# Part of the gram chains of images 1 to 5 moved from VectorE to ScalarE and GpSimd

## The chip, the cores and the metric

The kernel runs on one core of a Trainium2 chip. A core has five engines that run their own queues in order: TensorE (PE, matrix products into PSUM), VectorE (DVE), ScalarE (ACT), GpSimd (POOL) and SyncE (SP), which here only issues transfers. They wait for each other through semaphores. The metric is the device time of one execution in microseconds (us).

## The reference

A batch of 16 images of 64 channels and 128 x 128 pixels, in fp32, passes four layers of the form `x = x + f(gn(x))`, where `gn` is a group norm over 32 groups of two channels:

```
layer 0: f = conv_w @ (gram(v) @ v),  gram(v) = v v^T / (H W)   per image
layer 1: f = |scharr_x(v)| + |scharr_y(v)|                       3x3, per channel
layer 2: f = 3x3 convolution of the time-shifted v, plus bias
layer 3: f = clip(leaky(bn(conv1x1(conv3x3(v)))), 0, 255)        bn over all images
```

Layer 0 is linear in `x` once the 64 x 64 gram matrix of an image is known. So the kernel folds the norm, the gram product and `conv_w` into one 128 x 128 matrix (`abd`, two copies of a 64 x 64 block on the diagonal), and finds the statistics of the next norm (`co1`) from the gram matrix as well. That is a chain of small matrix products and small elementwise operations for each image, the gram chain. It must be done before layer 1 of the image can begin.

## The kernel before

**Stages.** The work is cut into steps of four quarters (`q` = 0 to 3). In a step each live stage does one slab of 16 of the 128 rows of one image. `Gram` (L407) loads `x` as `xr`, has ACT copy it into `xw` and sums the gram matrix into the PSUM tile `pg`. `Front` (L450) multiplies the image by `abd` on PE (`po`), normalizes it on ACT into `xh`, and does the Scharr filters of layer 1 (`sobel`, L527): on DVE `u` and `e` at the start of the quarters 0, four operations in quarter 1, one each in 2 and 3, with ACT's two `Abs` in between. `Layer2` (L625) normalizes its slab on ACT (`v`, in quarter 1), then POOL takes the border columns: four `edges` of 64 x 8 and two `v` of 128 x 9, also in quarter 1. In quarters 3 and 0 DVE forms a difference of rows (`d`), of which POOL's DMAs make shifted copies (`qd`). PE convolves: `one`, then the two halves of `two`, in quarters 2 and 3. DVE adds `edges` and `c` to `two` in quarter 0 of the next step. `Layer3` (L773) is alike, with ACT instead of POOL for `qd`.

**What runs when.** `starts` (L861) gives Front's image 0 step 15, Layer2's step 25 and Layer3's step 35, and each next image 8 steps more. The gram matrices of images 1 to 6 are made at double pace, one every 4 steps (L874), so they lie early, while Front works on images 0 to 2. `EARLY` is 3. In the last part, after the statistics of layer 3 are complete, the kernel reads all of `y` and `x3` again and writes the output.

**Order.** The stages record their instructions through `InOrder` (L63), which keeps each engine's instructions in program order; nearly all of them bear its line, L73, in the profile, so they are told apart by their tiles. At the end of each quarter `tick` (L252) lets every live chain go on to its next `yield`. A chain's operations of a quarter therefore stand in each engine's queue behind the stages' operations of that quarter.

**The gram chain** (L301) is a generator. One tick holds either PE's product or the small operations that follow from it; for image 1 (and 0) the yields under `if b > 1` fall away, so that both share a tick. `small_product` (L177) issues four small matmuls into `bank`, one PSUM bank that all chains share through `sm` (L187). The names in order: `gs` is `pg` out of PSUM; `g` the gram matrix of the image, with `st0` and `junk0` its means and squares; `rstd` (L257) makes the group's reciprocal deviation `r` (its `Sqrt`, `sd`, on ACT, the rest on DVE); `vv` holds vectors of means, `rw` their products as rows, `cs` the centred gram matrix, `rc` the scaled weights; `r2`, `wbd`, `ad` and `abd` are the folded matrix; `pp`, `av`, `pk`, `bias`, `st1` and `t` lead to the statistics of layer 0's output; `rstd` again, and `co` (the tile is `co1`) is what Front needs. `coefficients` (L278) is the shorter chain that layers 2 and 3 use, with the same `bank`. All small operations of both are on DVE before the change, apart from `sd`.

Of the kernel before, what the change touches and what calls it, by code (L numbers as in the profile page):

```python
# [12 lines left out]
ALU = mybir.AluOpType  # L13
AX = mybir.AxisListType

B, C, H, W = 16, 64, 128, 128
P = 128
HW = H * W
# [4 lines left out]
EARLY = 3  # L23
# [85 lines left out]
def tile_kernel(ctx: ExitStack, tc: tile.TileContext, x, cw_h, w2_t, b2, wbin_t, w1_t, b1, gamma, beta, consts, out):  # L109
    nc = tc.nc  # L110
    pe, dve, act, sp, pool = (InOrder(tc, e) for e in (nc.tensor, nc.vector, nc.scalar, nc.sync, nc.gpsimd))
# [9 lines left out]
    def k(name):  # L121
        return kc[:, AT[name][0]:AT[name][1]]

    def load_const(src, shape, name):
        t = cpool.tile(shape, F32, name=name)
        nc.sync.dma_start(t, src)
        return t

    cwh = load_const(cw_h, [P, C], "cwh")
# [39 lines left out]
    def sv(name, n=1):  # L169
        return small.tile([P, n], F32, tag=name, name=name)  # L170
# [6 lines left out]
    def small_product(dst, wt, src):  # L177

        for o in (1 - last[0], last[0]):
            pe.matmul(dst[cols(o)], wt[:, cols(o)], src, start=True, stop=True)  # L180
        last[0] = o
# [5 lines left out]
    def sm(n, rows=P):  # L187
        if n > 8:
            return bank[0:rows, P:P + n]
        turn[0] = (turn[0] + 1) % 16  # L190
        return bank[0:rows, 8 * turn[0]:8 * turn[0] + n]
# [9 lines left out]
    wbd = wpool.tile([P, P], F32, name="wbd")  # L201
# [55 lines left out]
    def rstd(mE, eps):  # L257

        me = sv("me", 2)
        dve.tensor_copy(me, mE)  # L260
        nv = sv("nv")
        dve.scalar_tensor_tensor(nv, me[:, 0:1], me[:, 0:1], me[:, 1:2], op0=ALU.mult, op1=ALU.subtract)
        var = sv("var")
        dve.tensor_scalar(var, nv, -1.0, eps, op0=ALU.mult, op1=ALU.add)
        sd = sv("sd")
        act.activation(sd, var, AF.Sqrt)
        yield
        r0 = sv("r0")
        dve.reciprocal(r0, sd)

        e = sv("e")
        dve.scalar_tensor_tensor(e, var, r0, r0, op0=ALU.mult, op1=ALU.mult)
        dve.tensor_scalar(e, e, -0.5, 1.5, op0=ALU.mult, op1=ALU.add)
        r = sv("r")
        dve.tensor_mul(r, r0, e)
        return r, me[:, 0:1]
# [23 lines left out]

    def gram_chain(b, pg):  # L301

        gs = stp.tile([P, C + 1], F32, tag="gs", name=f"gs_{b}", bufs=1)
        dve.tensor_copy(gs, pg)
        if b > 1:
            yield
        gd = sm(C + 1)
        small_product(gd, k("same"), gs)
        yield
        g = stp.tile([P, C + 1], F32, tag="g", name=f"g_{b}", bufs=1)  # L310
        dve.tensor_scalar_mul(g, gd, 1.0 / HW)
        mu = g[:, C:C + 1]
        st = sv("st0", 2)
        dve.tensor_copy(st[:, 0:1], mu)
        junk0 = stp.tile([P, C], F32, tag="junk0", name=f"junk0_{b}", bufs=1)
        dve.scalar_tensor_tensor(
            junk0, g[:, 0:C], 1.0, k("Id"), op0=ALU.mult, op1=ALU.mult, accum_out=st[:, 1:2]
        )
        if b > 1:
            yield  # L320
        pm = sm(2)
        small_product(pm, k("gavg"), st)
        yield
        r, mean = yield from rstd(pm, GN_EPS)

        vv = sv("vv", 5)
        dve.tensor_scalar_mul(vv[:, 0:1], mu, -1.0)
        dve.tensor_sub(vv[:, 1:2], mu, mean)
        dve.tensor_copy(vv[:, 2:3], mu)
        dve.tensor_sub(vv[:, 3:4], mu, mean)  # L330
        dve.tensor_scalar_mul(vv[:, 4:5], mean, -1.0)
        if b > 1:
            yield
        pr = sm(2 * P, rows=2)
        pe.matmul(pr[:, 0:P], vv[:, 0:2], k("hsame"), start=True, stop=True)
        pe.matmul(pr[:, P:2 * P], vv[:, 2:4], k("hsame"), start=True, stop=True)
        yield
        rw = stp.tile([2, 2 * P], F32, tag="rw", name=f"rw_{b}", bufs=1)
        dve.tensor_copy(rw, pr)
        if b > 1:  # L340
            yield
        pc = sm(C)
        pe.matmul(pc, rw[:, 0:P], rw[:, P:P + C], start=True, stop=True)
        yield

        cs = stp.tile([P, 2, C], F32, tag="cs", name=f"cs_{b}", bufs=1)
        for s in range(2):
            dve.tensor_add(cs[:, s, :], pc, g[:, 0:C])
        rc = stp.tile([P, C], F32, tag="rc", name=f"rc_{b}", bufs=1)
        dve.tensor_scalar(rc, cwh, r, 0.5, op0=ALU.mult, op1=ALU.mult)  # L350
        csf = cs.rearrange("p s c -> p (s c)")
        if b > 1:
            yield
        pq = sm(C)
        small_product(pq, csf, rc)
        yield
        r2 = sv("r2")
        dve.tensor_mul(r2, r, r)
        for s in range(2):
            rows = slice(s * C, (s + 1) * C)  # L360
            dve.tensor_scalar_mul(wbd[rows, rows], pq[rows], r2[rows])
        ad = stp.tile([P, C], F32, tag="ad", name=f"ad_{b}", bufs=1)
        dve.scalar_tensor_tensor(ad, pq, r2, k("Id"), op0=ALU.mult, op1=ALU.add)
        abd = stp.tile([P, P], F32, tag="abd", name=f"abd_{b}", bufs=EARLY + 3)
        dve.tensor_add(abd, wbd, k("I"))
        if b > 1:
            yield
        pd = sm(C + 3)
        small_product(pd[:, 0:C], csf, ad)
        small_product(pd[:, C:C + 2], abd, vv[:, 2:4])  # L370
        small_product(pd[:, C + 2:C + 3], wbd, vv[:, 4:5])
        yield
        pp = stp.tile([P, 2, C], F32, tag="pp", name=f"pp_{b}", bufs=1)
        for s in range(2):
            dve.tensor_mul(pp[:, s, :], pd[:, 0:C], ad)
        av = sv("av", 3)
        dve.tensor_copy(av, pd[:, C:C + 3])
        if b > 1:
            yield
        pk = sm(1)  # L380
        small_product(pk, pp.rearrange("p s c -> p (s c)"), k("q"))
        yield
        bias = sv("bias")
        dve.tensor_copy(bias, av[:, 2:3])
        st1 = sv("st1", 2)
        dve.tensor_add(st1[:, 0:1], av[:, 0:1], bias)
        t = sv("t1")
        dve.scalar_tensor_tensor(t, av[:, 1:2], av[:, 1:2], pk, op0=ALU.mult, op1=ALU.subtract)
        dve.scalar_tensor_tensor(
            st1[:, 1:2], st1[:, 0:1], st1[:, 0:1], t, op0=ALU.mult, op1=ALU.subtract  # L390
        )
        if b > 1:
            yield
        pm = sm(2)
        small_product(pm, k("gavg"), st1)
        yield
        r, mean = yield from rstd(pm, GN_EPS)

        co = stp.tile([P, 4], F32, tag="co1", name=f"co1_{b}", bufs=EARLY + 3)
        dve.tensor_copy(co[:, 0:1], r)  # L400
        dve.tensor_sub(co[:, 1:2], bias, mean)
        dve.tensor_mul(co[:, 1:2], co[:, 1:2], r)
        dve.reciprocal(co[:, 2:3], r)
        dve.tensor_copy(co[:, 3:4], mean)
        lead[b] = abd, co

    class Gram:  # L407
# [5 lines left out]
        def at(self, i, q):  # L413
# [29 lines left out]
            if n == 6:  # L443
                chains.append(gram_chain(b, self.pg))
# [466 lines left out]
    for step in range(steps):  # L911
        for q in range(4):
# [13 lines left out]
            for b in range(B):  # L926
                at, n = pace[b]
                for m in range(n):
                    v = 4 * n * (step - at) + n * q + m
# [101 lines left out]
```

## Time and profile before

| | |
|---|---|
| median of 3 runs | 2827.53 us (2825.04 to 2830.61) |
| the profiled execution's own time | 2829.05 us |
| its span | 2827.3 us |
| busy share of the span: PE, DVE, ACT, POOL | 79%, 78%, 75%, 31% |
| mean of one 128x1 operation of a chain on DVE | 0.13 to 0.16 us, issued 0.07 apart where independent |
| one large Scharr operation on DVE | 1.22 to 1.38 us |
| chains of images 1 to 5: `gs` at | 80.9, 128.4, 176.1, 236.7, 297.6 us |
| their last `co` at | 115.2, 186.7, 247.9, 310.5, 381.1 us |

The profile is of one execution. Its slices give each engine's busy share in tenths over 40 equal parts of the span, and below them the clock that the chip granted TensorE. A table of windows gives the same in microseconds between chosen times: length, then busy time and number of instructions for PE, PEld (weight loads), DVE, ACT and POOL, then PE's clock, the share in which the DMA engines were busy, and GB/s. The list of waits says which engine, before which tile, stood still for whom: the sum in us, how often, and the longest. A timeline has one row per instruction or run of equal ones: start, duration, engine, operation and tiles, and in brackets the idle time ahead of it and what ended it.

### The profile page before, as it was taken

The numbers are of one execution on the slowest core, as the hardware profiler recorded it, in microseconds if no ns is written. First come the engines' busy times: TensorE is split into PE (matmuls) and PEld (weight loads), VectorE is DVE, ScalarE is ACT, GpSimd is POOL, SyncE is SP. The second block draws the span as 40 slices with busy tenths as digits, with TensorE's granted clock in tenths as the row PEclk, the third lists the DMA queues.
The fourth block names the chain that finished last, engine by engine and source line by source line (L and its number), as shares of the span: only waits on it lengthen the run. The fifth ranks groups of instructions, "written<-read, shape, count | busy, mean of one in ns | idle before, by whom it ended". The sixth has DMA issues, their size and how long they took to land. (4 is left out here: it accounts for less than half of the span.)

```text
span 2827.3 us, 46297 instructions
## 1 busy us (share of the span) xinstructions
PE 2241.5 (79%) x14772; PEld 1157.1 (41%) x14772; DVE 2200.4 (78%) x3758; ACT 2120.5 (75%) x3171; POOL 884.3 (31%) x1326
## 2 busy tenths in 40 slices
PE   4568899999999999999999999999999995000000
PEld 2333444545453535363646363566666641000000
DVE  3999999898989898989898989999996434333332
ACT  4666779888888888888888888998997666333332
POOL 1035433343434343434343434454444300000000
PEclk8678999999999999999999999999999997555555
DMA  6788978888888888888888877888877668999999
GB/s 166 192 219 227 235 199 237 213 232 205 229 209 224 213 221 215 220 216 223 215 221 216 220 183 191 207 207 213 208 209 186 156 201 285 419 420 420 420 420 391
DMA packets 688880, 685.95 MB, mean 243 GB/s; under 512 B 61744, under 2 KB 590144, under 8 KB 688640
## 3 DMA queue, kind: packets, MB, share of 16 engines
q1 hardware_dynamic: 662656, 614.42, 73.7%
q0 software_dynamic: 24576, 68.12, 9.8%
q8 instruction: 119, 1.95, 0.3%
q14 instruction: 121, 0.99, 0.1%
q10 hardware_dynamic: 1408, 0.46, 0.1%
HBM read 346.23 MB, written 268.44 MB: 217 GB/s over the span
## 5 line engine op out<-in xcount | busy, mean ns | idle before, releaser
L73 PE MATMUL two<-d,w 128*64 128x508 f32 (+2 forms) x2560 | 894.2, 588 | 5.8 <-DVE d L73 5.8
L73 PE MATMUL two<-d,wi 128*64 128x508 f32 (+3 forms) x1536 | 620.1, 577 | 0.0
L73 POOL DMA_DIRECT2D qd<-d x512 | 269.8, 529 | 870.8 <-issue 318.4
L73 PE MATMUL two<-qd,pk 128*64 128x512 f32 (+1 forms) x1024 | 520.3, 589 | 3.2 <-DMA qd<-d 2.1
L73 POOL TENSOR_SCALAR edges<-v,co 64x8 f32<-64x8 f32 x512 | 348.8, 681 | 357.9 <-ACT v L73 248.7
L73 PEld LDWEIGHTS two<-d,w 128*64 128x64 f32 x2560 | 305.3, 136 | 285.5 <-issue 194.7
L73 PE MATMUL po<-x,abd 128*64 128x512 f32 x1024 | 369.8, 629 | 61.6 <-ACT xh L73 60.6
L73 DVE TENSOR_TENSOR d<-v 128x512 f32<-128x512 f32 (+1 forms) x512 | 345.9, 678 | 75.3 <-issue 36.0
L73 PE MATMUL one<-v,w 128*64 128x508 f32 (+2 forms) x1600 | 394.7, 578 | 0.0
L73 PE MATMUL one<-v,wi 128*64 128x508 f32 (+3 forms) x1536 | 391.4, 593 | 0.0
L73 ACT COPY qd<-d 64x512 f32<-64x512 f32 x512 | 315.3, 616 | 30.1 <-DVE d L73 23.7
L73 DVE SCALAR_TENSOR_TENSOR e<-e 128x1032 f32<-128x1032 f32 (+1 forms) x256 | 312.7, 1222 | 0.0
L73 ACT ACTIVATE xh<-po,co 128x128 f32<-128x128 f32 (+1 forms) x480 | 275.1, 621 | 40.8 <-PE po L73 38.8
L73 DVE SCALAR_TENSOR_TENSOR y<-two,c 128x1024 f32<-128x1024 f32 x128 | 155.8, 1217 | 132.0 <-ACT v L73 44.2
L73 PEld LDWEIGHTS two<-d,wi 128*64 128x64 f32 x1536 | 195.7, 136 | 145.2 <-issue 97.7
L73 POOL TENSOR_SCALAR v<-v,kc 128x9 f32<-128x9 f32 x256 | 249.7, 988 | 11.9
L73 PEld LDWEIGHTS one<-v,w 128*64 128x64 f32 x1600 | 171.9, 137 | 159.3 <-issue 97.5
L73 ACT ACTIVATE v<-x,co 128x512 f32<-128x512 f32 (+2 forms) x368 | 234.9, 704 | 0.0
L73 PEld LDWEIGHTS one<-v,wi 128*64 128x64 f32 x1536 | 163.0, 139 | 154.2 <-issue 110.1
L73 ACT ACTIVATE u<-u 128x1024 f32<-128x1024 f32 x128 | 135.5, 1058 | 96.7 <-DVE u L73 96.3
L73 DVE SCALAR_TENSOR_TENSOR u<-xh 128x1170 f32<-128x1170 f32 x128 | 175.5, 1371 | 12.2 <-ACT xh L73 9.8
L73 PEld LDWEIGHTS po<-x,abd 128*64 128x64 f32 x1024 | 110.8, 140 | 174.3 <-ACT xh L73 93.1
(154 smaller groups left out, 3476.0 us busy)
## 6 DMA issues: line engine op xcount, KB each, us to landing
xr<-in_x SPq DMA_DIRECT2D x128, 512.0 KB, 6.6
x<-in_x SPq DMA_DIRECT2D x256, 256.0 KB, 4.2
x_d<-u SPq DMA_DIRECT2D x512, 128.0 KB, 3.6
y_d<-y SPq DMA_DIRECT2D x512, 128.0 KB, 4.3
x_d<-x SPq DMA_DIRECT2D x496, 128.0 KB, 2.5
qd<-d POOLq DMA_DIRECT2D x256, 130.0 KB, 3.1
qd<-d POOLq DMA_DIRECT2D x256, 129.8 KB, 3.6
v<-x_d SPq DMA_DIRECT2D x448, 72.1 KB, 3.0
```

What stands on the lines that cost most here:

```text
L73: return self.tc.keep_in_program_order(call(*args, **kwargs))
```

## The change

For the chains of images 1 to 5 (`fill`; `2 * EARLY` is 6) the operations that read PSUM and are plain copies or scalings go to ACT: `gs`, `g`, `rw`, the two halves of `wbd`, `av`. Fifteen operations on small SBUF tiles go to POOL: `st0`, five of `vv`, `rc`, `r2`, `abd`, `bias`, the first half of `st1`, four of `co`. `junk0`, `cs`, `ad`, `pp`, `t`, the second half of `st1`, the reciprocal of `co` and all of `rstd` stay on DVE. The ticks and the order of the program are the same. The chains of image 0 and of images 6 to 15 are built as before.

```diff
...
 
     def gram_chain(b, pg):
 
+
+        fill = 1 <= b < 2 * EARLY
+        v, copy = (pool, act.copy) if fill else (dve, dve.tensor_copy)
+
+        def scaled(dst, src, by):
+            if fill:
+                act.mul(dst, src, by)
+            else:
+                dve.tensor_scalar_mul(dst, src, by)
+
         gs = stp.tile([P, C + 1], F32, tag="gs", name=f"gs_{b}", bufs=1)
-        dve.tensor_copy(gs, pg)
+        copy(gs, pg)
         if b > 1:
             yield
         gd = sm(C + 1)
         small_product(gd, k("same"), gs)
         yield
         g = stp.tile([P, C + 1], F32, tag="g", name=f"g_{b}", bufs=1)
-        dve.tensor_scalar_mul(g, gd, 1.0 / HW)
+        scaled(g, gd, 1.0 / HW)
         mu = g[:, C:C + 1]
         st = sv("st0", 2)
-        dve.tensor_copy(st[:, 0:1], mu)
+        v.tensor_copy(st[:, 0:1], mu)
         junk0 = stp.tile([P, C], F32, tag="junk0", name=f"junk0_{b}", bufs=1)
         dve.scalar_tensor_tensor(
             junk0, g[:, 0:C], 1.0, k("Id"), op0=ALU.mult, op1=ALU.mult, accum_out=st[:, 1:2]
...
         r, mean = yield from rstd(pm, GN_EPS)
 
         vv = sv("vv", 5)
-        dve.tensor_scalar_mul(vv[:, 0:1], mu, -1.0)
-        dve.tensor_sub(vv[:, 1:2], mu, mean)
-        dve.tensor_copy(vv[:, 2:3], mu)
-        dve.tensor_sub(vv[:, 3:4], mu, mean)
-        dve.tensor_scalar_mul(vv[:, 4:5], mean, -1.0)
+        v.tensor_scalar_mul(vv[:, 0:1], mu, -1.0)
+        v.tensor_sub(vv[:, 1:2], mu, mean)
+        v.tensor_copy(vv[:, 2:3], mu)
+        v.tensor_sub(vv[:, 3:4], mu, mean)
+        v.tensor_scalar_mul(vv[:, 4:5], mean, -1.0)
         if b > 1:
             yield
         pr = sm(2 * P, rows=2)
...
         pe.matmul(pr[:, P:2 * P], vv[:, 2:4], k("hsame"), start=True, stop=True)
         yield
         rw = stp.tile([2, 2 * P], F32, tag="rw", name=f"rw_{b}", bufs=1)
-        dve.tensor_copy(rw, pr)
+        copy(rw, pr)
         if b > 1:
             yield
         pc = sm(C)
...
         for s in range(2):
             dve.tensor_add(cs[:, s, :], pc, g[:, 0:C])
         rc = stp.tile([P, C], F32, tag="rc", name=f"rc_{b}", bufs=1)
-        dve.tensor_scalar(rc, cwh, r, 0.5, op0=ALU.mult, op1=ALU.mult)
+        v.tensor_scalar(rc, cwh, r, 0.5, op0=ALU.mult, op1=ALU.mult)
         csf = cs.rearrange("p s c -> p (s c)")
         if b > 1:
             yield
...
         small_product(pq, csf, rc)
         yield
         r2 = sv("r2")
-        dve.tensor_mul(r2, r, r)
+        v.tensor_mul(r2, r, r)
         for s in range(2):
             rows = slice(s * C, (s + 1) * C)
-            dve.tensor_scalar_mul(wbd[rows, rows], pq[rows], r2[rows])
+            scaled(wbd[rows, rows], pq[rows], r2[rows])
         ad = stp.tile([P, C], F32, tag="ad", name=f"ad_{b}", bufs=1)
         dve.scalar_tensor_tensor(ad, pq, r2, k("Id"), op0=ALU.mult, op1=ALU.add)
         abd = stp.tile([P, P], F32, tag="abd", name=f"abd_{b}", bufs=EARLY + 3)
-        dve.tensor_add(abd, wbd, k("I"))
+        v.tensor_add(abd, wbd, k("I"))
         if b > 1:
             yield
         pd = sm(C + 3)
...
         for s in range(2):
             dve.tensor_mul(pp[:, s, :], pd[:, 0:C], ad)
         av = sv("av", 3)
-        dve.tensor_copy(av, pd[:, C:C + 3])
+        copy(av, pd[:, C:C + 3])
         if b > 1:
             yield
         pk = sm(1)
         small_product(pk, pp.rearrange("p s c -> p (s c)"), k("q"))
         yield
         bias = sv("bias")
-        dve.tensor_copy(bias, av[:, 2:3])
+        v.tensor_copy(bias, av[:, 2:3])
         st1 = sv("st1", 2)
-        dve.tensor_add(st1[:, 0:1], av[:, 0:1], bias)
+        v.tensor_add(st1[:, 0:1], av[:, 0:1], bias)
         t = sv("t1")
         dve.scalar_tensor_tensor(t, av[:, 1:2], av[:, 1:2], pk, op0=ALU.mult, op1=ALU.subtract)
         dve.scalar_tensor_tensor(
...
         r, mean = yield from rstd(pm, GN_EPS)
 
         co = stp.tile([P, 4], F32, tag="co1", name=f"co1_{b}", bufs=EARLY + 3)
-        dve.tensor_copy(co[:, 0:1], r)
-        dve.tensor_sub(co[:, 1:2], bias, mean)
-        dve.tensor_mul(co[:, 1:2], co[:, 1:2], r)
+        v.tensor_copy(co[:, 0:1], r)
+        v.tensor_sub(co[:, 1:2], bias, mean)
+        v.tensor_mul(co[:, 1:2], co[:, 1:2], r)
         dve.reciprocal(co[:, 2:3], r)
-        dve.tensor_copy(co[:, 3:4], mean)
+        v.tensor_copy(co[:, 3:4], mean)
         lead[b] = abd, co
 
     class Gram:
```

In the built program the order on PE and SP is the same as before, instruction by instruction. On ACT, `gs` stands behind two copies of `xw` and before `xh`; `g` behind a copy of `xw` and before the two `Abs`; `rw` and `wbd` behind two `xh`; `av` behind the square of the slab and before `v`. In chain 1 `g` stands behind the square of the slab, `rw` and `wbd` behind a copy of `xw`, `av` behind two `xh`. On POOL, in chains 3 to 5, the order of one chain among the stages' work is:

```
edges x4, v x2, co x4 of the chain before, st0, qd x2, qd x2, vv x5, edges x4, v x2, qd x2, qd x2,
rc, edges x4, v x2, r2, abd, qd x2, qd x2, edges x4, v x2, bias, st1, qd x2, qd x2, ...
```

In chains 1 and 2 no `edges`, `v` or `qd` lie between, but for one set of `edges` and `v` before `bias` of chain 2. On DVE, `ad` waits for ACT, beside PE and POOL.

## The prediction

> **What bounds the kernel now.** I read three things, from coarse to fine. First the slices of the page, which say where one engine is full:
>
> ```profile
> PE   4568899999999999999999999999999995000000
> DVE  3999999898989898989898989999996434333332
> ACT  4666779888888888888888888998997666333332
> PEclk8678999999999999999999999999999997555555
> ```
>
> A slice is 70.7 us. VectorE (DVE) is full in slices 2 to 5 while TensorE (PE) is at 5 to 8; from slice 6 (about 350 us) PE is full at full clock. The five chains of images 1 to 5 run from 80.9 us (first `gs`) to about 381 us (last `co`), so the change lies in the stretch in which DVE sets the pace. The same cut finer, with each engine's busy time, then the granted PE clock:
>
> ```profile
> 80.00:120.00 40.00, 18.02 (x134) 7.82 (x130) 37.02 (x74) 26.62 (x37) 0.20 (x1) 0.59 0.66 167
> 120.00:167.00 47.00, 26.87 (x371) 15.70 (x369) 43.91 (x77) 31.72 (x46) 0.20 (x1) 0.66 0.84 202
> 167.00:240.00 73.00, 60.56 (x656) 30.03 (x652) 67.08 (x125) 45.89 (x63) 43.35 (x50) 0.91 0.92 235
> 240.00:305.00 65.00, 54.59 (x515) 26.80 (x516) 60.41 (x128) 45.88 (x68) 32.07 (x42) 0.89 0.95 239
> 305.00:370.00 65.00, 58.56 (x496) 26.27 (x494) 57.41 (x117) 52.31 (x78) 30.30 (x40) 0.95 0.84 217
> 370.00:430.00 60.00, 60.00 (x316) 23.42 (x314) 58.07 (x122) 50.01 (x81) 21.96 (x32) 1.00 0.79 206
> ```
>
> DVE (third) is busy 93% and more until 305 us, PE (first) is close behind from 167 us on, and GpSimd (POOL, fifth), idle before 167 us, then has a half to 60% of its time taken. What a delay of PE costs there is nearly what a delay of DVE costs. What DVE waits for between 80 and 380 us:
>
> ```profile
> DVE gs L73 <- PE pg L73: 6.8, 5, 1.8
> DVE d L73 <- POOL v L73: 5.9, 5, 1.6
> DVE d L73 <- issue: 2.7, 1, 2.7
> DVE u L73 <- ACT u L73: 2.6, 2, 1.3
> ```
>
> So the only engine it repeatedly waits for within a step is POOL, whose `edges` and `v` come once per step. Last, the timeline of DVE, POOL and PE in one step of chain 3:
>
> ```profile
> 196.68 0.14 DVE L73 TENSOR_SCALAR vv<-me 128x1 f32<-128x1 f32 x1
> 196.74 1.23 DVE L73 SCALAR_TENSOR_TENSOR u<-u 128x1040 f32<-128x1040 f32 x1
> ...
> 202.58 0.41 DVE L73 COPY rw<-bank 2x256 f32<-2x256 f32 x1
> ...
> 205.50 0.69 DVE L73 TENSOR_TENSOR d<-v 128x512 f32<-128x512 f32 x1 [1.31 <-POOL v L73]
> ```
> ```profile
> 196.34 1.03 POOL L73 DMA_DIRECT2D qd<-d  x2 [4.52 <-issue]
> 197.40 7.35 POOL L73 TENSOR_SCALAR edges<-v,co 64x8 f32<-64x8 f32 x4
> 204.84 0.62 POOL L73 TENSOR_SCALAR v<-v,kc 128x9 f32<-128x9 f32 x2
> ```
> ```profile
> 196.68 1.01 PE L73 MATMUL bank<-kc,vv 128*2 128x128 f32 x4 [3.33 <-DVE vv L73]
> 197.63 3.82 PE L73 MATMUL one<-v,wi 128*64 128x512 f32 x12
> ```
>
> Four `edges` of 64x8 take 7.35 us, though the fastest of the 60 in 160 to 400 us took 0.303 (median 1.143, slowest 4.168). They are stretched under the DVE stream of 1.2 us operations and fast once DVE stands still: the two `v` at 204.84, in DVE's gap, took 0.62 together. And PE was standing still for `vv`, in front of a whole convolution step.
>
> **What the Trainium skill says.** "SBUF — State Buffer", Who interferes with whom: an instruction of DVE with two SBUF inputs contends with a GpSimd instruction that reads SBUF, and the one issued second blocks until the first ends. The trace agrees for POOL (1.143 against 0.303 us); the DVE rows show no loss (`u<-u` 1.219 to 1.237). "PSUM — Partial Sum Buffer", PSUM bank collisions raise a hardware error: two engines on one bank and quadrant need an order, reads included. All chain products lie in one bank, and in the built program DVE's `ad` now waits for ScalarE's (ACT) `wbd`, which it doesn't read. Before, DVE did both; no run yet shows the price. "ScalarE: Activation LUTs", What ACT_TABLE_LOAD costs, gives the price of an ACTIVATE: 186 ns, 0.833 per element, 93 per pointer operand. An estimate for `g` is 0.24 us, for half a `wbd` 0.33; `xh<-pe` (128, two pointers) took 0.45 against 0.48 so computed.
>
> **What it removes.** DVE slots, start to start, in chain 2: `gs` 0.21, `g` and `st0` 0.32, five `vv` 0.32, `rw` 0.33, `rc` 0.16, `r2` 0.26, two `wbd` 0.61, `abd` 0.20, `av` 0.07, `bias` and `st1` 0.26, four `co` 0.40: 3.14 us, 15.7 for five chains. The durations add up to more, since these rows overlap.
>
> **What it adds.** ACT gets 6 instructions per chain, some 2 us, and had 11 to 15 us idle per window above: its own time is hidden, but not its place in line. POOL gets 15 per chain. Each costs 0.33 us with DVE still, 1.14 and more under the stream, and stands behind what is in POOL's queue. The new waits:
>
> *Chains 1 and 2.* ACT's `gs` stands behind two copies of `xw`, which wait for the gram matmuls and for a load: in chain 1 the second ran 82.92 to 84.1. Then `gs` (84.3), the product, `xh` twice and the square (1.1 + 1.0 us), `g` at 86.7: DVE's `junk0` waits till then, and the four Sobel operations start at 86.9, not 84.06: +2.8. The other savings of the chain return 2.6, a wait for POOL's `st1` costs 0.4: +0.6. In chain 2 `junk0` waits for `g` till 137.5 and DVE's next large one for ACT's `u` behind it: +1.1; `ad` waits for `wbd` behind `xh`, 162.35 instead of 161.31; then `st1` on POOL stands behind six `edges` and `v` that end at 175.45 where DVE wanted it at 173.9: +1.3. Less the savings, both chains come to **+2**.
>
> *Chains 3 to 5, each.* (A) POOL: four `co` and `st0` behind `v` (end 187.1 in chain 3). DVE's mean needs PE's product of `st0`. Two of the five pass under the stream before DVE stands still at 189.6, the rest in 0.33 each: mean at 191.6 instead of 190.37, **+1.3**. (B) Five `vv` between the `qd` DMAs (end 197.4) and `edges`. Before, the fifth POOL operation from there ended at about 205.2 (0.33 into `v`); with DVE's gap coming 0.65 earlier I take 204.5. PE's product starts then, not at 196.68, then `one` (3.8) and the two halves of `two` (4.3, from 201.28 to `po` at 205.56) end at about 213.3. DVE wanted `two` at 208.55: **+4.7**. In chain 4 DVE wants it 2.9 after it is ready, so +4.3; in chain 5 4.7, but PE is full from 320 us on and its own 6 us count, I take +5. POOL's `v` itself comes only 0.6 late, since POOL catches up while DVE stands. (C) `rc` delays PE's product by 3 us, which `two` just bears (needed at 222.68); `r2` behind `edges` and `v` comes at 218.6, then `wbd` on ACT, 0.7, then `ad` at 219.4 instead of 217.92, its savings back: **+1.3**. (D) `st1` behind `v`: **+0.3**. Sum of the three: 7.6, 7.2, 7.9 less 0.2 each for `gs`: 22.1.
>
> Against this, DVE no longer stands for `gs` (6.8 us in all). Behind a late PE most of that is gone, but I credit 4. 2 + 22 - 4 = **+20 us**. From 350 us PE is full and its order is fixed; nothing there gives the delay back, and the tail after 2340 us starts later by as much. The profiled execution took 2829.05 (span 2827.3); +20 is 2849.1. It lies 1.5 above the median 2827.53, so the forecast is **2848**.
>
> **Unknown costs.** A 128x1 operation on POOL: 0.33 (as `v` in a gap) to 2.3 us (two DVE operations); I take about 1.4 under the stream. A semaphore hop: nothing to 0.1, I take 0.1. `ad` behind `wbd`: 0 to 1.5 per chain. At the low ends B falls to about 1, A to 0, C to 0.5. At the high ends B is 8, A 2, C 3. A gain from overlap can't exceed the 3.14.
>
> **Rivals.** *DVE is simply relieved* (all on the other side): the chain is off the path, its consumers sit a tick later, and the bound engine loses 15.7 us of work. 2811.8. For it: DVE is 93% busy, a tick lies between most pairs. Against: (B)'s 3.33 us PE wait says that the chain is on PE's path. It decides if POOL's five `vv` end within 2.5 us, the slack of `two`. *POOL is cheap*: its small operations slip in between at 0.33 to 0.6, and waits and savings cancel: -3 to +6, 2829. For it: DVE's own short operations open gaps. Against: 60 `edges` with a median of 1.143. *PE falls out of its clock*: `one` took 2.78 us at full clock, 5.32 after a 2.46 us wait at 211.35, so 8 us waits in each of three chains cost 2 to 3 us more in each of several steps, and the high ends of B and C hold: +40, 2868. For it: clock 0.59 in 80 to 120 us, where PE is half idle.
>
> **How the numbers follow.** Forecast (2837 to 2860) 0.60; PE's clock (2860 to 2885) 0.17; POOL cheap (2823 to 2837) 0.15; relief 0.08. Leaving out relief, a little of the cheap case and the upper half of the clock case gives 2830 to 2868. 0.2% is 5.7 us, about what a measurement of this kernel can tell from no change. The cheap case gives 0.12 within and 0.03 above: faster 0.08, same 0.12, slower 0.80.
>
> **What would show it.** PE's wait before the product with `vv` 6 to 8 us instead of 3.3, its releaser POOL; DVE waiting for PE `two` after it in chains 3 and 4; `ad` waiting for ACT or POOL; `junk` for ACT `g` in chains 1 and 2; POOL's `vv` near 1 us each; everything after 400 us as before but 20 us later. The forecast is wrong if `vv` run at 0.3 us under the stream, or if PE makes good its wait before 350 us.

## The result, and the profile after

| | before | after |
|---|---|---|
| median (4 runs each, side by side) | 2827.29 us | 2847.0 us (2845.09 to 2849.91) |
| ratio after to before | | 1.0067, 95% interval 1.0055 to 1.0079 |
| profiled execution, its span | 2829.05, 2827.3 us | 2845.09, 2843.3 us |

The kernel became 0.67% slower, 19.7 us by the medians. The slices of the page after, tenths of an engine's time over 40 equal parts of the span:

```profile
PE   3567899999999999999999999999999995000000
DVE  3887889898989898989898989999997434333332
...
PEclk7679899999999999999999999999999998555555
```

The nines of VectorE (DVE) in slices 2 to 6 have become eights and one seven, and TensorE (PE) has lost nothing from slice 6 on. So DVE was relieved of work, and the stretch got longer all the same. The table of windows of the kernel after (length; then busy time and count of PE, PEld, DVE, ScalarE (ACT), GpSimd (POOL); PE clock, DMA share, GB/s), in the three windows of the chains 3 to 5:

```profile
167.00:240.00 73.00, 54.49 (x600) 27.07 (x598) 60.00 (x94) 44.33 (x66) 40.27 (x59) 0.85 0.84 216
240.00:305.00 65.00, 49.97 (x410) 21.44 (x407) 50.73 (x95) 41.89 (x65) 32.55 (x54) 0.89 0.90 215
305.00:370.00 65.00, 54.91 (x412) 23.87 (x409) 55.95 (x98) 50.30 (x77) 36.81 (x56) 0.92 0.84 218
```

DVE is now idle for 13.0, 14.3 and 9.1 us there; before it was 5.9, 4.6 and 7.6. Part of that is the work that left, the rest is standing. What it stands for, in the waits of DVE from 80 to 400 us of the kernel after (sum in us, times, longest):

```profile
DVE d L73 <- issue: 10.5, 2, 5.4
DVE ad L73 <- ACT wbd L73: 8.4, 4, 2.6
DVE junk L73 <- ACT g L73: 6.5, 2, 4.9
DVE st L73 <- POOL st L73: 5.2, 3, 2.0
DVE d L73 <- PE two L73: 4.1, 3, 2.7
DVE two L73 <- PE two L73: 3.7, 3, 1.9
DVE me L73 <- PE bank L73: 3.1, 3, 1.3
```

Of these lines only the `issue` of `d` (2.7 us) and the wait at `two` (0.4) had their like before; the waits for `gs`, 6.8 us before, are down to one of 1.8 us. And the waits of PE in the same stretch:

```profile
PE bank L73 <- POOL st L73: 13.5, 5, 5.1
PE bank L73 <- POOL vv L73: 12.9, 6, 2.8
...
PE bank L73 <- POOL rc L73: 7.9, 2, 4.4
```

In chains 3 and 4 three products now wait for POOL (`st0`, `vv`, `rc`), in the other chains one or two. In chain 3 this looks as follows. The timeline of POOL in the kernel after (start, duration, operation; idle time and releaser in brackets):

```profile
201.37 0.35 POOL L73 TENSOR_SCALAR vv<-g 128x1 f32<-128x1 f32 x1
201.70 1.12 POOL L73 TENSOR_TENSOR vv<-g,me 128x1 f32<-128x1 f32 x1
202.77 1.19 POOL L73 COPY vv<-g 128x1 f32<-128x1 f32 x1
203.92 1.18 POOL L73 TENSOR_TENSOR vv<-g,me 128x1 f32<-128x1 f32 x1
205.06 0.22 POOL L73 TENSOR_SCALAR vv<-me 128x1 f32<-128x1 f32 x1
205.26 3.43 POOL L73 TENSOR_SCALAR edges<-v,co 64x8 f32<-64x8 f32 x4
...
219.86 2.13 POOL L73 TENSOR_SCALAR rc<-cwh,r 128x64 f32<-128x64 f32 x1
221.99 3.28 POOL L73 TENSOR_SCALAR edges<-v,co 64x8 f32<-64x8 f32 x4
```

PE in the same stretch of the kernel after:

```profile
202.88 0.59 PE L73 MATMUL bank<-kc,vv 128*2 128x128 f32 x2 [2.83 <-POOL vv L73]
205.15 0.59 PE L73 MATMUL bank<-kc,vv 128*2 128x128 f32 x2 [1.68 <-POOL vv L73]
205.67 4.51 PE L73 MATMUL one<-v,wi 128*64 128x512 f32 x12
...
211.72 1.02 PE L73 MATMUL two<-d,wi 128*64 128x508 f32 x4
...
222.05 0.48 PE L73 MATMUL bank<-rc,cs 128*64 128x64 f32 x4 [4.43 <-POOL rc L73]
```

And DVE:

```profile
212.83 0.69 DVE L73 TENSOR_TENSOR d<-v 128x512 f32<-128x512 f32 x1 [5.10 <-issue]
...
226.92 0.28 DVE L73 SCALAR_TENSOR_TENSOR ad<-bank,r,kc 128x64 f32<-128x64 f32 x1 [2.62 <-ACT wbd L73]
```

The five `vv` take 3.9 us on POOL; those in the middle last as long as one large DVE operation each. `one` starts at 205.67 instead of 197.63, and DVE stands 5.1 us at `d`. The profile names no releaser there ("issue"); I read it as PE's late `two`, whose first half reads the buffer that `d` writes. By the trace that half ends at 212.74, and `d` begins at 212.83; in chain 4 and in run 5 below the distance is 0.09 us too.

**The yardstick.** Both traces hold the same large DVE operations in the same order, so each has a lag: how much later than before it begins. The lag counts from the Scharr pass `u<-xh` at 69.4 us of the kernel before, ahead of the chains, so that the loads of image 0 (2.2 us of difference between these two traces) stay out. The places where DVE's lag of the kernel after changes by 0.6 or more in chain 3, computed from start times in both traces (before, after, change):

```
187.02  189.92  -0.72  junk<-g,kc    g and st0 no longer on DVE
190.37  194.33  +1.02  me<-bank      PE's product of st0
205.50  212.83  +3.81  d<-v          PE's product of vv
217.92  226.92  +1.83  ad<-bank      ACT's wbd
219.63  229.66  +1.24  d<-v          PE's two, behind the product of rc
231.59  242.86  +1.56  st<-st,t      POOL's st1
234.15  244.20  -1.22  d<-v          POOL's v, now no longer waited for
```

By chain the lag grows by 1.5 (chains 1 and 2), 6.3 (3), 6.6 (4) and 3.0 us (5), to 17.4. From there to 2320 us it stays between 17.2 and 18.4: the delay arises in the chains, and the steps behind them do not make it good. In the last part the distance between these two executions falls to 13.8. It falls there by 1.6 to 3.7 us in eleven of the twelve runs below as well (in run 2 it rises by 1.1), so this is at least in part a slow last part of the one execution before. The lag leaves that scatter out, and against the times of the runs below it was off by up to 2.5 us, run 11 apart. It is of one execution all the same: PE's clock can move it by about 2 us (run 8 below), so differences of that size between two lags say nothing by themselves.

### The profile page after: what moved, and what is told of

It reads as the page before. It is cut to its first block, busy times and chain, and to the rows that moved or that the text cites. A ratio compares the mean times of both kernels' runs of the same rounds, so it can differ in the third digit from the quotient of the medians.

```text
span 2843.3 us, 46325 instructions
## 1 busy us (share of the span) xinstructions
PE 2244.9 (79%) x14772; PEld 1179.3 (41%) x14772; DVE 2188.3 (77%) x3653; ACT 2127.4 (75%) x3201; POOL 907.8 (32%) x1401
## 3 DMA queue, kind: packets, MB, share of 16 engines
q8 instruction: 119, 1.95, 0.3%
## 5 line engine op out<-in xcount | busy, mean ns | idle before, releaser
L73 POOL TENSOR_SCALAR edges<-v,co 64x8 f32<-64x8 f32 x512 | 338.5, 661 | 317.6 <-ACT v L73 247.7
L73 POOL TENSOR_SCALAR v<-v,kc 128x9 f32<-128x9 f32 x256 | 243.3, 964 | 12.0
L73 PEld LDWEIGHTS pg<-xw 128*64 128x64 f32 x4096 | 163.0, 144 | 48.2 <-issue 40.3
```

What stands on the lines that cost most here:

```text
L73: return self.tc.keep_in_program_order(call(*args, **kwargs))
```

## The experiments

The lags after 400 us of all runs, beside the times; "before" is the kernel before in the same series, and a count in brackets tells how many executions a median rests on:

| kernel | lag, us | time, us | before, us |
|---|---|---|---|
| the changed kernel | 17.4 | 2847.0 (4) | 2827.3 (4) |
| 1 ACT's part alone | 3.3 | 2830.0 (14) | 2827.2 (17) |
| 2 POOL's part alone | 20.3 | 2845.5 (4) | 2827.2 (17) |
| 3 `vv` back on DVE | 13.3 | 2841.7 (1) | 2827.2 (17) |
| 4 `r2` back on DVE | 20.6 | 2845.8 (1) | 2827.2 (17) |
| 5 `vv` alone on POOL | 5.7 | 2833.6 (1) | 2825.5 (1) |
| 6 `vv`, `co`, `st0` back | 8.2 | 2835.2 (1) | 2825.5 (1) |
| 7 `r2` back, `ad` first | 23.3 | 2850.2 (1) | 2825.5 (1) |
| 8 `vv` early on POOL | 12.4 | 2838.6 (1) | 2825.5 (1) |
| 9 as 7, `rc` back too | 17.7 | 2844.1 (1) | 2828.1 (25) |
| 10 three copies on ACT alone | -0.3 | 2825.6 (13) | 2828.1 (25) |
| 11 as 10, `vv` early on POOL | 4.1 | 2826.1 (13) | 2828.1 (25) |
| 12 as 8, `rc`, `r2` early too | 6.6 | 2831.2 (12) | 2826.8 (15) |

### 1 and 2: which engine makes the loss

```diff
-        v, copy = (pool, act.copy) if fill else (dve, dve.tensor_copy)
+        v, copy = dve, act.copy if fill else dve.tensor_copy
```

> Only the six operations per chain that go to ScalarE are moved; the fifteen of GpSimd are on VectorE as before the change. Theory (the loss is made by GpSimd's place in line, ScalarE costs only at g in chains 1 and 2 and at ad): 2824 to 2829 us, no slower than before; junk0 still waits for g in chains 1 and 2, and PE's wait before the product with vv is no longer than the 3.3 us of before. Rival (ScalarE's place in line makes most of the loss): 2840 or more. Rival (moves to ScalarE are free): 2820, the 7.4 us of VectorE time saved.

Measured: ratio 1.0015 (1.0007 to 1.0024), so not free, and 1 us above the range of the theory. DVE's lag rises by 4.1 and 1.8 at `st0` in chains 1 and 2 (ACT's `g`), and by 0.7, 0.7, 1.6 and 1.6 at and behind `ad` in chains 1 to 4 (ACT's `wbd`), and falls by 2.1, 1.1, 2.1 and 0.9 at `gs` in chains 1, 2, 4 and 5.

```diff
-        v, copy = (pool, act.copy) if fill else (dve, dve.tensor_copy)
+        v, copy = pool if fill else dve, dve.tensor_copy
...
         def scaled(dst, src, by):
-            if fill:
-                act.mul(dst, src, by)
-            else:
-                dve.tensor_scalar_mul(dst, src, by)
+            dve.tensor_scalar_mul(dst, src, by)
```

> Only the fifteen operations per chain that go to GpSimd are moved. Theory: 2842 to 2847 us, nearly all of the loss: GpSimd's vv, st0, rc, r2 and st1 come late in chains 3 to 5 whatever ScalarE does. Rival (ScalarE's place in line makes most of the loss): 2827 or less. Rival (the two parts are harmful only together, through ad waiting for r2 and wbd in a row): 2830 to 2838.

Measured: ratio 1.0071 (1.0056 to 1.0086). POOL's part makes the whole loss by itself. `d` costs 4.7 in chain 3 and 3.2 in chain 4, and `ad` is 1.7 late in both, though here DVE does `wbd` itself and waits for POOL's `r2` instead.

### 3 and 4: one step of the forecast undone

The five `vv` (3), or `r2` (4), go back to DVE:

```diff
-        v.tensor_scalar_mul(vv[:, 0:1], mu, -1.0)
-        v.tensor_sub(vv[:, 1:2], mu, mean)
+        dve.tensor_scalar_mul(vv[:, 0:1], mu, -1.0)
+        dve.tensor_sub(vv[:, 1:2], mu, mean)
...
```
```diff
-        v.tensor_mul(r2, r, r)
+        dve.tensor_mul(r2, r, r)
```

> The change with the five vv on VectorE again. Theory: vv is the largest single term; VectorE's stop at the difference d in chains 3 and 4 (3.8 and 4.1 us more than before) goes, and PE's wait for GpSimd before the product with vv; 8 us less than the change, 2839. Rival (GpSimd is simply overloaded in this stretch and the lateness moves to the next operation in its queue): at most 2 us less, 2845 or more.

> The change with r2 on VectorE again, so that ScalarE's wbd and VectorE's ad no longer wait for GpSimd's queue; the order of ad behind wbd in the shared PSUM bank stays. Theory (the queue behind edges and v makes ad late): ad's wait in chains 3 to 5 falls from about 2 to under 1 us each, 3 us less in all, 2844. Rival (the order in the bank and ScalarE's own queue make it late): 1 us less or nothing, 2846 or more.

Measured: with `vv` back the lag fell from 17.4 to 13.3, half of the 8 us that were expected. With `r2` back nothing was gained: `ad` was still 1.7 and 1.6 late in chains 3 and 4, and the lag is 3.2 larger, of which 2.1 stand at a `two` in chain 3, behind PE's wait for `st0`, where PE came out at half clock. With `r2` on POOL and `wbd` on DVE (run 2) it was 1.7 late too. So two delays of nearly one size lie beside each other at `ad`: POOL's `r2` behind `edges`, and ACT's `wbd` behind two `xh`. Either alone is enough.

### 5 and 6: how large B and A are

`vv` alone on POOL, all else as in the kernel before (5); the edit is against the changed kernel:

```diff
-        v, copy = (pool, act.copy) if fill else (dve, dve.tensor_copy)
+        v, copy, vvp = dve, dve.tensor_copy, pool if fill else dve
...
         def scaled(dst, src, by):
-            if fill:
-                act.mul(dst, src, by)
-            else:
-                dve.tensor_scalar_mul(dst, src, by)
+            dve.tensor_scalar_mul(dst, src, by)
...
-        v.tensor_scalar_mul(vv[:, 0:1], mu, -1.0)
-        v.tensor_sub(vv[:, 1:2], mu, mean)
+        vvp.tensor_scalar_mul(vv[:, 0:1], mu, -1.0)
+        vvp.tensor_sub(vv[:, 1:2], mu, mean)
...
```

The changed kernel with `vv`, `co` and `st0` on DVE (6), beside the edit of run 3:

```diff
-        v.tensor_copy(st[:, 0:1], mu)
+        dve.tensor_copy(st[:, 0:1], mu)
...
-        v.tensor_copy(co[:, 0:1], r)
-        v.tensor_sub(co[:, 1:2], bias, mean)
+        dve.tensor_copy(co[:, 0:1], r)
+        dve.tensor_sub(co[:, 1:2], bias, mean)
...
```

> The kernel before with only the five `vv` of the chains of images 1 to 5 on GpSimd; the rest of the small operations is on VectorE. If the forecast's step B has its size (TensorE's product 8 us late, of which 4.3 to 5 reach VectorE in chains 3, 4 and 5, less 1.0 us of VectorE time a chain), the steps after 400 us are 9 to 13 us later than in the kernel before: about 2838. If the `vv` are only one of several delays that lie beside each other (moving them back alone brought 4 of 8), a chain loses 1 to 2.5 and the steps are 3 to 7 later: about 2832. If GpSimd serves them without harm, -4 to 0: 2823 to 2827.

> The changed kernel with `vv`, the four small operations of `co` and the one of `st0` back on VectorE. With `vv` alone back the steps after 400 us were 13.3 us behind the kernel before. If step A (`co` and `st0` behind `v`) costs what the traces show at `me` (1.0 us in each of chains 3, 4, 5) and hides the rest of B (TensorE waited for `st0` up to 5.1 us where it no longer waited for `vv`), they are 7 to 10 behind: 2834 to 2837. If A lies beside other work, they stay 12 to 13.5 behind: about 2840.

Measured: 5.7, the second case of the three, and 8.2, the first case of the two. The timeline of PE in chain 3 with `vv` alone on POOL:

```profile
199.97 0.58 PE L73 MATMUL bank<-kc,vv 128*2 128x128 f32 x2 [5.90 <-POOL vv L73]
202.24 0.59 PE L73 MATMUL bank<-kc,vv 128*2 128x128 f32 x2 [1.69 <-POOL vv L73]
202.75 4.92 PE L73 MATMUL one<-v,wi 128*64 128x512 f32 x12
```

Here PE stands for `vv` for 7.6 us, as the forecast had it, because nothing else held it up earlier. DVE's `d` comes 4.1 late, and still the three chains lose only 3.0, 2.0 and 1.9 us (chains 1 and 2 gain 1.2): later waits get shorter by what the earlier one took. In the changed kernel PE has already stood for `st0` (1.8, 3.3 and 5.1 us in chains 3 to 5), so its wait for `vv` is shorter. From run 3 to run 6, `co` and `st0` bring 5.1 us, more than the 3.4 that stand at `me` in chains 3 to 5. The rest is found at the `two` behind `me`: in run 3 DVE stands there 2.0 us in chain 4, since PE, behind its wait for `st0`, worked at half clock (0.50 from 258.4 to 263.6 us). Run 6 has no such wait, and the changed kernel doesn't either, so 2 of the 5.1 us hang on the clock.

### 7 and 9: what really holds `ad` and the `d` behind it

```diff
-        v.tensor_mul(r2, r, r)
+        dve.tensor_mul(r2, r, r)
+        ad = stp.tile([P, C], F32, tag="ad", name=f"ad_{b}", bufs=1)
+        dve.scalar_tensor_tensor(ad, pq, r2, k("Id"), op0=ALU.mult, op1=ALU.add)
         for s in range(2):
             rows = slice(s * C, (s + 1) * C)
             scaled(wbd[rows, rows], pq[rows], r2[rows])
-        ad = stp.tile([P, C], F32, tag="ad", name=f"ad_{b}", bufs=1)
-        dve.scalar_tensor_tensor(ad, pq, r2, k("Id"), op0=ALU.mult, op1=ALU.add)
```

> The changed kernel with `r2` back on VectorE and `ad` issued ahead of the two `wbd`, so that VectorE reads the bank before ScalarE does. If two delays of one size lie beside each other (GpSimd's late `r2`; ScalarE's `wbd` behind its two `xh` and ahead of `ad` on the bank), both are gone now and `ad` comes on time: 1.8 us in each of chains 3 and 4, 0.8 in 5, 0.7 in 2, so 4 to 6 less than the changed kernel, 11.5 to 13.5 behind the kernel before: 2839 to 2841. If the late product on the bank (`rc` on GpSimd) is what `ad` waits for, it stays at 17 and `ad` stands for TensorE: about 2845.

Measured: 23.3, worse than the changed kernel, and neither theory said so. `ad` itself was on time (0.6 gained in every chain), but the lag rose at the next wait. In the waits of DVE of this kernel:

```profile
DVE d L73 <- issue: 14.7, 4, 5.9
...
DVE me L73 <- ACT wbd L73: 2.9, 2, 1.9
```

In chain 3 `d` behind `ad` came 4.1 late instead of 1.2: PE had been standing 4.4 us for POOL's `rc`, and DVE's wait at `ad` had only covered it. Run 9 adds one edit:

```diff
-        v.tensor_scalar(rc, cwh, r, 0.5, op0=ALU.mult, op1=ALU.mult)
+        dve.tensor_scalar(rc, cwh, r, 0.5, op0=ALU.mult, op1=ALU.mult)
```

> The kernel of the run before (the changed kernel with `r2` on VectorE and `ad` ahead of `wbd`, whose steps after 400 us were 23.3 us behind the kernel before) with `rc` back on VectorE as well. Theory: TensorE's stand for GpSimd's `rc` (4.4 us in chain 3) and VectorE's wait at `ad` lay beside each other; with `ad` on time VectorE stood at `d` for TensorE's late `two` instead (+4.1 in chain 3, +3.2 at the end of 4, +3.1 in 5). With `rc` back these go too: 8 to 11 less, 12 to 15 behind, 2838 to 2842. Rival: `wbd`'s place on ScalarE behind the two `xh` makes `abd` and so TensorE late by itself: 20 to 23 behind, 2846 to 2850.

Measured: 17.7, so 5.6 less, between the two. The `d` in chain 3 lost its delay (0.5 instead of 4.1), which settles `rc` as its cause there. The two other places that the expectation named stayed: in chain 4 the late `d` is that of `vv` (3.3), and in chain 5 the 3.1 stand at layer 3's `y`. What else stayed is seen in chain 4 of this kernel, in the timelines of DVE and ACT:

```profile
294.26 0.16 DVE L73 COPY me<-bank 128x2 f32<-128x2 f32 x1 [1.95 <-ACT wbd L73]
```
```profile
292.61 1.11 ACT L73 ACTIVATE xh<-po,co 128x512 f32<-128x512 f32 x2
293.61 0.62 ACT L73 ACTIVATE wbd<-bank,r 64x64 f32<-64x64 f32 x2
```

This `me` belongs to a chain of `coefficients`. It reads other columns of `bank` and needs nothing of `wbd`, yet it waits for ACT to be done there. The order on the bank was only handed on from `ad` to the next reader. POOL kept `vv`, `co` and `st0` in this kernel, and the `d` of `vv` in chain 3 is 4.3 late in it. Run 7 is 6 us above the changed kernel; a part of that arises in chain 1, where DVE stands for ACT's `u` 1.7 longer behind the new order, and the rest I can't put down to one wait. It stays open.

### 8 and 12: the same engines, another place in the queue

```diff
     def rstd(mE, eps, then=None):
...
         dve.tensor_copy(me, mE)
+        if then is not None:
+            then(me[:, 0:1])
...
-        r, mean = yield from rstd(pm, GN_EPS)
-
         vv = sv("vv", 5)
-        v.tensor_scalar_mul(vv[:, 0:1], mu, -1.0)
+
+        def early(mean):
+            v.tensor_scalar_mul(vv[:, 0:1], mu, -1.0)
...
+        r, mean = yield from rstd(pm, GN_EPS, early)
```

> The changed kernel with the five `vv` issued on GpSimd right behind `me`, one tick earlier, ahead of the square root; they need nothing but `mu` and the mean. If the loss of B is a matter of where they stand in GpSimd's order (behind `r`, with TensorE waiting), they are done before TensorE asks, and this is worth as much as having them on VectorE (4 us) and about 1 us a chain of VectorE time besides: 12 to 14 behind the kernel before, 2839 to 2842. If GpSimd is late at that earlier place too (behind `v`), or `vv` under VectorE's stream takes so long that `edges` come later in turn, 16 to 20 behind: 2844 to 2847.

Measured: 12.4, as good as `vv` back on DVE (13.3). `d` in chains 3 and 4 no longer came 3.8 and 4.1 late but 0.3 early, and its wait has a named releaser now, POOL's `v` as before. This fits how I read "issue". PE in chain 3 of this kernel:

```profile
199.87 0.60 PE L73 MATMUL bank<-kc,vv 128*2 128x128 f32 x4
...
217.27 0.48 PE L73 MATMUL bank<-rc,cs 128*64 128x64 f32 x4 [5.60 <-POOL rc L73]
```

No wait for `vv` at all, but a longer one for `rc`. And of the 8.6 us that `d` won in the two chains, 3.2 came back at the `two` behind `me` (1.1 and 2.1). The main cause is PE's clock. In chain 4 PE stands for `st0` equally long in the changed kernel and in this one, and goes on at different speeds; PE of the changed kernel, then PE and DVE of run 8:

```profile
261.73 0.28 PE L73 MATMUL bank<-st,kc 128*64 128x2 f32 x4 [3.31 <-POOL st L73]
261.87 0.62 PE L73 MATMUL two<-d,wi 128*64 128x512 f32 x1
```
```profile
257.65 0.38 PE L73 MATMUL bank<-st,kc 128*64 128x2 f32 x4 [3.29 <-POOL st L73]
257.88 1.09 PE L73 MATMUL two<-d,wi 128*64 128x512 f32 x1
...
263.25 0.38 DVE L73 TENSOR_TENSOR two<-two,edges 128x8 f32<-128x8 f32 x2 [1.99 <-PE two L73]
```

The granted clock was 1.00 from 261.8 to 265.2 us there and 0.50 from 257.8 to 263.0 us here. What decides between them no run shows. The next edit, against the wait for `rc`, issues `rc` and `r2` right behind `r`, a round of `edges` and `v` earlier:

```diff
         r, mean = yield from rstd(pm, GN_EPS, early)
+        rc = stp.tile([P, C], F32, tag="rc", name=f"rc_{b}", bufs=1)
+        v.tensor_scalar(rc, cwh, r, 0.5, op0=ALU.mult, op1=ALU.mult)
+        r2 = sv("r2")
+        v.tensor_mul(r2, r, r)
```

> The changed kernel with the same operations on the same engines, but three groups issued on GpSimd as soon as their inputs are known: the five `vv` right behind `me` (that alone left 12.4 us after 400 us, of 17.4), and now `rc` and `r2` right behind `r`, one round of `edges` and `v` earlier. TensorE stood 5.6 us for `rc` in chain 3 with `vv` early, then `d` came 1.9 late and `ad` 1.8. If the loss is one of GpSimd's place in the order, TensorE no longer waits for `rc`, `d` after `ad` comes on time, and `ad` keeps only ScalarE's share (1.6): 7 to 10 behind the kernel before, 2834 to 2838. If the new place costs as much, since `edges` are then 2.3 us later for `two`, or since GpSimd's operations are slow wherever they stand, 12 to 15 behind: 2839 to 2842.

Measured: lag 6.6, ratio to the kernel before 1.0015 (1.0007 to 1.0024), better than either expectation. The timelines of POOL and PE in chain 3:

```profile
199.70 1.39 POOL L73 TENSOR_SCALAR rc<-cwh,r 128x64 f32<-128x64 f32 x1
201.07 1.14 POOL L73 TENSOR_TENSOR r<-r 128x1 f32<-128x1 f32 x1
202.19 4.36 POOL L73 TENSOR_SCALAR edges<-v,co 64x8 f32<-64x8 f32 x4
```
```profile
213.11 0.48 PE L73 MATMUL bank<-rc,cs 128*64 128x64 f32 x4 [2.56 <-DVE cs L73]
```

`rc` is there 12 us ahead of its use, and PE waits for DVE's `cs` as its last input. POOL does the same 15 operations per chain. They did become a little shorter at their new places (the five `vv`, `rc` and `r2` of chain 3 together 5.5 us, 6.2 in the changed kernel), too little to explain it. So three quarters of what the change cost by the medians (4.4 us are left of 19.7) came of their place in POOL's queue.

### 10 and 11: a version that may beat both

Only `gs`, `rw` and `av` go to ACT (10), and `vv` early to POOL besides (11, with the edit of run 8 and `vvp` of run 5):

```diff
-        v, copy = (pool, act.copy) if fill else (dve, dve.tensor_copy)
+        v, copy = dve, act.copy if fill else dve.tensor_copy
...
         def scaled(dst, src, by):
-            if fill:
-                act.mul(dst, src, by)
-            else:
-                dve.tensor_scalar_mul(dst, src, by)
+            dve.tensor_scalar_mul(dst, src, by)
```

> A version that may beat both: only the three copies out of PSUM (`gs`, `rw`, `av`) on ScalarE in chains 1 to 5; `g`, `wbd` and everything that GpSimd had stay on VectorE. From the traces: `gs` gives 2.1, 1.1, 2.1 and 0.9 in chains 1 to 4, of which `two` takes back 1.3 in chain 3 and little in 4; `rw` 0.3 and `av` 0.2 a chain; the losses at `junk` (+4.1, +1.8) and at `ad` (0.7 to 1.6 a chain) belonged to `g` and `wbd` on ScalarE and are gone. Together 4 to 8 us less than the kernel before: 2819 to 2823. Rival: `gs` behind two `xw` copies on ScalarE makes `g` late for VectorE instead, and TensorE stands for `gs` (3.9 us in chains 3 and 4): no gain, 2826 to 2830.

> The same with the five `vv` on GpSimd, issued right behind `me`. In the changed kernel this placement took away the 3.8 and 4.1 us at `d` in chains 3 and 4, and `vv` off VectorE gave 0.35 a chain. If nothing new waits: 1 to 2 below the version with the copies alone. Rival: GpSimd's five operations under VectorE's stream (3.9 us) make its `edges` late for `two` in chains 3 to 5: 0 to 5 above it.

Measured: both have the ratio 0.9993 (0.9985 to 1.0001), about 2 us below the kernel before and not told apart from it; the gain of 4 to 8 us that was expected did not come. In chain 4 of run 10 the gain and its loss stand together, in the timeline of DVE and then of ACT:

```profile
239.01 0.38 DVE L73 TENSOR_TENSOR two<-two,edges 128x8 f32<-128x8 f32 x2 [1.86 <-PE two L73]
```
```profile
236.51 2.23 ACT L73 COPY xw<-xr 128x1024 f32<-128x1024 f32 x2 [3.08 <-PE pg L73]
238.63 0.20 ACT L73 COPY gs<-pg 128x65 f32<-128x65 f32 x1
```

DVE no longer stands for `gs`: its lag falls by 2.1. Two operations later it stands for `two`, 1.9 of it, and the lag is where it was. DVE had been waiting for PE at `gs`, and PE is no earlier. In chain 1 `g` takes back 2.7, behind `gs`, which ACT does after the `xw` copies. Run 11's profiled execution lay 5.5 us above its median, so nothing is read from its lag: 6.7 us of it arise in chain 4, where DVE stands for ACT's `u` behind slabs whose loads came late. Its median is not told apart from that of run 10.

```profile
278.99 1.35 ACT L73 ACTIVATE v<-v,co 128x1154 f32<-128x1154 f32 x1 [6.90 <-DMA x_d<-x]
```

## Why the prediction was right, and where not

The direction and the size held: +20 was forecast, 17.4 is the lag and 19.7 the difference of the medians (the two profiled executions lie 16.0 apart). The nearness of the sum is in part luck, as the terms show. By chain:

```
                     forecast          lag in the trace
chains 1 and 2       +2                +1.5
chain 3              +7.6              +6.3
chain 4              +7.2              +6.6
chain 5              +7.9              +3.0
credit for gs        -4                (within the rows above)
```

- **Chains 1 and 2** went as described: `junk` waits for ACT's `g` (6.5 us in two waits), and `st` for POOL's `st1` in chain 2.
- **A** (+1.3): 1.0, 1.0 and 1.3 at `me`, PE waiting for POOL's `st0`. Right as seen from DVE. Not seen was that PE's stand there, up to 5.1 us, also shortens its next wait, and that PE can come out of it at half clock.
- **B** (+4.7, +4.3, +5): 3.8 and 4.1 in chains 3 and 4, and nothing at that place in chain 5, where the lag falls by 0.7. DVE stops at `d`, three operations ahead of the `two` that the forecast named, because `d` writes what the late `two` still reads. PE's wait was not 6 to 8 us in one piece but 2.83 and 1.68, as `vv` arrives in two pairs and PE was late already; `one` behind it took 4.5 and 4.8 us, for which the forecast had 3.8. For chain 5 the term "PE is full from 320 us on and its own 6 us count" was mis-sized: PE waited there 5.05 us for `st0` and then 1.26 for `vv`, and DVE's losses stand at `me`, at the next `two` (0.9) and at layer 3's `y` (1.9). And the sum over waits overstated what B is worth: moving `vv` early brought 5.0 in all (17.4 to 12.4), against the 7.9 that stand at `d`.
- **C** (+1.3): this step failed. It held that PE's delay by `rc` is one "which `two` just bears" and that `r2`'s place sets `ad`. In the trace `ad` and the `d` behind it cost 3.1 in chain 3, `ad` alone 1.8 in chain 4 and 0.8 in chain 5. Run 4 showed that `r2` is not needed for it, run 9 that `rc`, 2.13 us long on POOL and waited for 4.4 us by PE, makes the `d` of chain 3 late, and the step from run 8 to run 12 that `rc` and `r2` together are worth 5.8 us.
- **D** (+0.3): +1.56 and then -1.22 in chain 3, so 0.3; in chain 4 +1.57 and -0.61, so 1.0.
- **The credit for `gs`** (-4): too much. Chain 4 got 2.1 and gave 2.0 to `two`, chain 5 got 0.9 and gave 0.6, and what chains 1 and 2 got was in their +2 already. Without the credit the forecast would have been +24. So errors cancelled: B was 6.1 too large in sum, and the credit for `gs` 3.6 too large the other way; C (1.8) and the `two` and `y` of chain 5 (2.7) cost more than forecast.

Two readings of the windows were inexact, without effect on the sum: DVE is busy 92% and more until 305 us, and ACT had 10 to 27 us idle per window, not 11 to 15.

Of the rivals, "DVE is simply relieved" fell with the waits of PE. "POOL is cheap" was right on many durations: in the kernel after the five `st0` took 0.185 to 0.242 us and 13 of the 20 `co` 0.19 or less. It was wrong on what they cost, since their place in the queue does the harm. "PE falls out of its clock" was right in part: the clock was 0.85, 0.89 and 0.92 in the three windows, against 0.91, 0.89 and 0.95, and stretches of half clock behind PE's stands reached DVE in runs 3, 4, 8 and 12. The +40 did not come; how much of the 19.7 is the clock's no run separates.

The Trainium skill's price of an ACTIVATE ("ScalarE: Activation LUTs", What ACT_TABLE_LOAD costs) gave 0.24 us for `g` and 0.33 for half a `wbd`; the trace has medians of 0.228 and 0.309. Its rule that two engines on one bank need an order, reads included ("PSUM — Partial Sum Buffer", PSUM bank collisions raise a hardware error), was the part without a price. Runs 1 and 4, where `ad` doesn't wait for `r2`, give one for this kernel: 1.6 to 1.7 us at `ad` in chains 3 and 4 and less in the others; in run 9 it is 1.95 at the `me` that comes next. ACT's two reads took 0.62 us, hardly more than the 0.58 that they took on DVE; the rest is ACT's place in line.

## What to carry to other kernels

An operation moved to an idle engine takes its place in that engine's queue: before asking how long it takes there, ask what stands ahead of it and who waits behind it, and issue it as soon as its inputs exist (here that was worth three quarters of the loss). Time taken off the busiest engine is worth nothing at a place where that engine waits for another one anyway. When several waits lie beside each other, undoing one may show too little and adding them up too much; only runs that undo them together tell their worth.

## What the runs showed of the hardware

- A 128x1 operation of POOL takes 0.18 to 0.24 us where DVE stands still or runs short operations, and mostly 1.12 to 1.19 in a DVE stream of operations with two inputs in SBUF, the length of about one of them; a few in that stream took 0.19 to 0.35. Beside DVE's `y<-two,c`, which reads one input from PSUM, `bias` and `st1` took 0.187 and 0.191 (379 us). A 128x64 `rc` takes 0.35 to 2.43.
- DVE loses less. Beside POOL's 128x1 operations at most 0.04 us shows, and `u<-u` of 128x1040 keeps its median of 1.23 us in the kernel after. Beside the larger `rc` and `abd` single operations get longer: in the kernel before no `u<-u` of 128x1024 between 80 and 400 us took more than 1.222, in the kernel after one took 1.34 beside `rc`, and one 1.47 that began just behind `abd`:

```profile
103.16 0.67 POOL L73 TENSOR_TENSOR abd<-wbd,kc 128x128 f32<-128x128 f32 x1 [2.15 <-issue]
```
```profile
103.44 1.47 DVE L73 TENSOR_TENSOR u<-u 128x1024 f32<-128x1024 f32 x1
```

  That agrees with the Trainium skill ("SBUF — State Buffer", Who interferes with whom), by which the order of issue decides which side waits.
- A matmul of 128x512 is recorded with 0.59 to 0.62 us at a granted clock of 1.00 and with 1.05 to 1.09 at 0.50. Behind a stand of 3.3 us the clock was 1.00 in one execution and 0.50 in another.
- In these programs, splitting a chain that lives in one PSUM bank over DVE and ACT made DVE's next reader of that bank wait for ACT's queue (`ad`, 0.7 to 1.8 us in chains 2 to 5 of the kernel after), in run 9 a reader of other columns from another chain (`me`, 1.95 us).
